# Self-attention products moved behind the scores, into the scores' PSUM ring

## The chip, the cores and the metric

The kernel runs on one core of one Trainium2 chip. A core has five engines with queues of their own: TensorE (PE) multiplies matrices into PSUM, VectorE (DVE), ScalarE (ACT) and GpSimd (POOL) work elementwise, and SyncE (SP) issues DMAs. Each engine executes its own queue in order; between engines semaphores order the work. [...] The metric is the time of one execution on the device in microseconds (us), the median of several runs; less is better.

## The reference

A decoder block in float32, on x of 8 x 224 x 512 and a context of 8 x 750 x 384: self-attention, cross-attention, feed-forward, each with a residual and a layer norm behind it. The change touches the self-attention only:

```python
x = _rmsnorm(tokens, norm_w)
q = x @ Wq
k, v = jnp.split(x @ Wkv, 2, axis=-1)
q, k, v = (split(q), split(k), split(v))      # 16 heads of 64
q = _head_rmsnorm(q, q_gamma)                 # q / max(|q|, 1e-12) * (gamma + 1) * 8
k = _head_rmsnorm(k, k_gamma)
sim = jnp.einsum('bhid,bhjd->bhij', q, k)
sim = jnp.tanh(sim / SOFTCLAMP) * SOFTCLAMP   # 50
attn = jax.nn.softmax(sim * DIM_HEAD ** (-0.5), axis=-1)
out = jnp.einsum('bhij,bhjd->bhid', attn, v)
return out.reshape(b, n, HEADS * DIM_HEAD) @ Wo
x = _layernorm(x + attention)
```

The norm of a head runs over its 64 elements. With the tanh at 50 and the scale of 1/8 the exponent is bounded, so the kernel takes exponentials with no maximum.

## The kernel before

The self-attention works in *slots*, one for each pass of `for m in range(NS)`: NS = 32. Slot m = 8 g + hp handles two batches (group g, G = 448 rows, halves u = 0 and 1 of S = 224) and one pair of heads hp. Within a slot PE does, in program order:

- `self_values(m - 1)` (matmuls on line 577, tile `ov`): exponentials of the slot before by values.
- `self_scores(m)` (line 507, tile `sc_a`): scores of the pair, for each u in a tile of 2 x 512 float32, two banks, from the pool `a_sc`, which has two such buffers. ACT then runs tanh (line 517) and exp (line 523), each in two pieces of keys a half: eight calls.
- `project_v` (line 484, `mm_v`): one tile of values, in 24 of the 32 slots. ACT copies it out (line 494) in one to four pieces, as the row tiles of 128 straddle batches of 224.
- `transpose_xn` (line 342, `tr_x`): a tile of the next group's normalised input, in ten slots. DVE copies it out (`copy_xn`, line 346).
- `products_qk(m + 2)` (line 421; `q_x`, `q_z`, `q_w`): queries and keys for two slots later.
- `self_output` (line 610, `mm_o`): an output tile of the group before, in the slots that the table `out_at` names.

Queries and keys are not computed as one product of 448 x 512 by 512 x 256, but with seven products of half blocks, in `half_products` (Winograd's form): inputs and weights are cut into blocks, POOL prepares four sums of each (`sum_input` line 405, `sum_weights` line 385), and the products accumulate into three PSUM tiles x, z, w. ACT copies an intermediate state out of x three times (`m1` line 259, `u2` line 265, `u4` line 271), before the next product may add to it, and z and w once (c11 line 263, c22 line 269); POOL adds m1 to c11 (line 272) and u4 to c22 (line 273). After a yield, two last products follow, with DVE's c21 (line 278) and ACT's c12 (line 282). x, z and w come from the pool `a_mm`, three banks, which `mm_v`, `tr_x` and `mm_o` use too.

The head norms of queries and keys: ACT squares (`square_qk`, line 447), DVE sums within heads (`head_norms`, lines 454 to 465), POOL takes the power -0.5 (tile `nm_i`, line 167), DVE spreads the result and scales (`scale_qk`, lines 472 and 474). In slot m `head_norms(m + 1)` comes before `scale_qk(m + 1)`; the scores of slot m + 1 need both. `inverse_sums(m)` sums the exponentials on DVE (lines 532 to 563), `weigh(m - 1)` (line 590) scales the values' result.

POOL also computes the sums of weights for each hp (at set slots, `sums_at`), of the inputs of the next group (hp = 5), and, in `room_sums`, of cross-attention weights (line 138). From slot 10 on the blocks of weights come from DRAM with `load_slot`, issued two slots ahead; `room_load` brings in cross-attention weights.

The order of PE, DVE, ACT and POOL instructions is that of the program text (`manual_schedule`). SP's DMAs are placed by the scheduler.

The function `half_products` is also used by the cross-attention, with `third` set and no calls to deal out.

Of the kernel before, what the change touches and what calls it, by code (L numbers as in the profile page):

```python
# [21 lines left out]
F32 = mybir.dt.float32  # L22
# [17 lines left out]
P = 128  # L40
# [24 lines left out]
def decoder_block(ctx: ExitStack, tc: tile.TileContext, a: dict, out: bass.AP):  # L65
# [175 lines left out]

    def half_products(product, a, b, sums_a, sums_b, dest, parts, acc, third=None):

        (a11, a12), (_, a22) = a
        (b11, _), (b21, b22) = b  # L250
        s1, s2, s3, s4 = sums_a
        t1, t2, t3, t4n = sums_b
        c11, c12, c21, c22 = (dest(r, c) for r in range(2) for c in range(2))
        m1, u2, u4 = parts
        x_, z_, w_ = acc
        if third:
            a13, a23, b31, b32, dif = third
        product(x_, a11, b11, True)
        nc.scalar.copy(m1, x_)  # L259
        product(z_, a12, b21, True)  # L260
        if third:
            product(z_, a13, b31, False)
        nc.scalar.copy(c11, z_)
        product(x_, s2, t2, False)
        nc.scalar.copy(u2, x_)
        product(w_, s3, t3, True)
        if third:
            product(w_, a23, b32, False)
        nc.scalar.copy(c22, w_)
        product(x_, s1, t1, False)  # L270
        nc.scalar.copy(u4, x_)
        nc.gpsimd.tensor_tensor(c11, c11, m1, ALU.add)
        nc.gpsimd.tensor_tensor(c22, c22, u4, ALU.add)
        yield
        product(w_, a22, t4n, False)
        if third:
            product(w_, a23, dif, False)
        nc.vector.tensor_tensor(c21, w_, u2, ALU.add)  # L278
        product(x_, s4, b22, False)
        if third:  # L280
            product(x_, a13, b32, False)
        nc.scalar.copy(c12, x_)
        yield
# [15 lines left out]
    with tc.tile_pool(name="a_sb", bufs=2) as sb, tc.tile_pool(  # L299
# [38 lines left out]
        def transpose_xn(i):  # L338
            y = xn.pop(i)
            trs[i] = tr = ps_mm.tile([P, KD, P], F32, tag="mm", name="tr_x")  # L340
            for k in range(KD):
                nc.tensor.transpose(tr[:, k, :], y[:, k * P : (k + 1) * P], ident)
# [80 lines left out]
                    skip_group_check=True,  # L423
                )

        def products_qk(m):
            g, hp = divmod(m, NPAIR)
            qk[m] = sb.tile([P, 2, G], F32, name="qk", bufs=3)
            if m < NPAIR + 2:
                q, k = ([w[:, 2 * kh : 2 * kh + 2, hp * P : (hp + 1) * P] for kh in range(2)]  # L430
                    for w in (wq, wk))
                b = (q[0], None), (q[1], k[1])
                t = [work[:, hp % 4, i] for i in range(4)]
            else:
                w7 = stream[:, m % 2]
                b = (w7[:, 0], None), (w7[:, 1], w7[:, 2])
                t = [w7[:, 3 + i] for i in range(4)]
            return half_products(
                product_qk, input_blocks(g), b, [sums_x[:, i] for i in range(4)], t,
                lambda u, w: qk[m][:, w, u * S : (u + 1) * S],  # L440
                [sb.tile([P, S], F32, name=n, bufs=1) for n in ("qm1", "qu2", "qu4")],
                [ps_mm.tile([P, S], F32, tag="mm", name=f"q_{n}") for n in ("x", "z", "w")],
            )

        def square_qk(m):
# [3 lines left out]
        def head_norms(m):  # L449

            quarter = sb.tile([P, 4 * NB], F32, name="nm_q", bufs=1)
            nc.vector.tensor_reduce(
                quarter, sq_qk[m].rearrange("p w (b c) -> p (w b) c", c=Q32), AX.X, ALU.add,
                apply_transpose=True,
            )
            other = sb.tile([P, 4 * NB], F32, name="nm_o", bufs=1)
            for q in range(P // Q32):
                o = q ^ 1  # L460
                nc.vector.tensor_copy(
                    other[q * Q32 : (q + 1) * Q32], quarter[o * Q32 : (o + 1) * Q32]
                )
            nc.vector.tensor_tensor(quarter, quarter, other, ALU.add)
            nc.vector.tensor_scalar(quarter, quarter, 1e-24, None, ALU.max)  # L465
            inv[m] = sb.tile([P, 2, 2 * NB, 1], F32, name="nm_i")
            rsqrt(inv[m].rearrange("p w b o -> p (w b o)"), quarter)
# [27 lines left out]

        def self_scores(m):

            qT, kT = qk[m][:, 0], qk[m][:, 1]
            scs = []
            for u in range(2):  # L500
                sc = ps_sc.tile([P, 2, 512], F32, name="sc_a")
                sc = sc[:, :, 0 : NT * S].rearrange("p j (t q) -> p j t q", t=NT)
                scs.append(sc)
                for kt, (k0, n) in enumerate(KEYS):
                    for j in range(2):
                        h0, c = j * DH, u * S
                        nc.tensor.matmul(  # L507
                            sc[:n, j, kt, :],
                            lhsT=kT[h0 : h0 + DH, c + k0 : c + k0 + n],
                            rhs=qT[h0 : h0 + DH, c : c + S],  # L510
                            start=True,
                            stop=True,
                        )
            for u in range(2):
                pr, sc = prs[u], scs[u]
                for kt, (_, n) in enumerate(KEYS):
                    nc.scalar.activation(  # L517
                        pr[:n, :, kt], sc[:n, :, kt], AF.Tanh, scale=1.0 / SOFTCLAMP
                    )


                for kt, (_, n) in enumerate(KEYS):
                    nc.scalar.activation(  # L523
                        pr[:n, :, kt], pr[:n, :, kt], AF.Exp, scale=SOFTCLAMP * SCALE
                    )

        def inverse_sums(m):

# [2 lines left out]
            for u in range(2):  # L531
                nc.vector.tensor_reduce(  # L532
                    quarter[:, u, :, :, :, 0].rearrange("p j b t -> p j t b"),
                    prs[u].rearrange("p j t (b c) -> p j t b c", c=Q32),
                    AX.X, ALU.add, apply_transpose=True,
                )


            flat = quarter.rearrange("p u j b t g -> p (u j b t) g")
# [145 lines left out]

        nc.vector.tensor_scalar(gscale, gam, 1.0, DH**0.5, ALU.add, ALU.mult)
        head_norms(0)
        project_v(0, 0)
        project_v(1, 0)
        project_qk(1)  # L690
# [1 line left out]
        head_norms(1)  # L692
        for i in opened[0][2:]:
            project_v(i, 0)
        for i in range(4):
            if i < 2:
                sum_input(0, 2 * i)
                sum_input(0, 2 * i + 1)
            sum_weights(2, i)

        out_at = [(), (2, 3, 5), (0, 2, 4, 6), (3, 4, 5)]

        sums_at = {0: (3,), 1: (4,), 2: (5, 6), 3: (7,), 4: (0,), 6: (1,)}
        for m in range(NS):
            g, hp = divmod(m, NPAIR)
            ahead = opened[g + 1] if g + 1 < NG else ()
            if m > 0:
                self_values(m - 1)
            self_scores(m)

            c = 1 - hp // 4
            tiles = opened[g + hp // 4] if g + hp // 4 < NG else ()
            if hp % 4 < len(tiles):
                project_v(tiles[hp % 4], c)
            turned = ahead[hp - 2] if 2 <= hp < 2 + len(ahead) else None

            behind = turned is not None and turned * P % (2 * G) < G < turned * P % (2 * G) + P
            if turned is not None and not behind:
                transpose_xn(turned)
            for i in due:  # L720
                scales.append(layernorm([i]))
            due.clear()
            if 2 <= m + 1 < NS and m > 0:
                head_norms(m + 1)
            if m > 0:
                weigh(m - 1)
            if turned is not None and not behind:
                copy_xn(turned)
            sums = inverse_sums(m)
            next(sums)  # L730
            products = products_qk(m + 2) if m + 2 < NS else iter(())
            next(products, None)
            if m + 1 < NS:
                scale_qk(m + 1)
            for _ in products:
                pass
            if m + 2 < NS:
                square_qk(m + 2)
            if behind:
                transpose_xn(turned)  # L740
                copy_xn(turned)
            for f in scales:
                f()
            scales.clear()
# [6 lines left out]
            if hp < len(ahead):  # L751
                square(ahead[hp])
                rms_norms(ahead[hp], ahead[hp] + 1)
            if hp == 5 and ahead:
                for i in range(4):
                    sum_input(g + 1, i)
            for p in sums_at.get(m, ()):
                for i in range(4):
                    sum_weights(p, i)
            if m == NPAIR - 1:  # L760
                stream = wpool.tile([P, 2, 7, KD // 2, P], F32, tag="w", name="w_slot")
                load_slot(m + 3)
# [1 line left out]
                room_load(0)  # L764
            if m >= NPAIR - 1 and m + 4 < NS:
                load_slot(m + 4)

            for _ in range({9: 2, 10: 3, 12: 2, 13: 3}.get(m, 0)):
                next(room_steps[m // 12])
            if m == 10:  # L770
                room_load(1)
            if m == NS - 3:
                xw = wpool.tile([P, 2, KC + 2 + NSUM, P], F32, tag="w", name="xw")
# [728 lines left out]
```

## Time and profile before

| what | value |
|---|---|
| median of 3 runs | 1697.95 us (1697.94 to 1701.26) |
| the profiled execution | 1700.17 us, its span 1698.4 us |
| granted TensorE clock, mean | 0.995 |
| PE busy | 1637.3 us, 96% |
| DVE, ACT, POOL busy | 1339.9, 983.8, 895.1 us |
| self-attention's slots | from 39.19 us to about 553 us of the span |
| DMA, mean | 88 GB/s |

In the profile PE is the matmul pipeline and PEld its loading of weights, which overlaps it; ACTq and the like are the sequencers. A row of a timeline gives start and duration in us, engine, line, operation, tiles as `out<-in`, shapes and how many; in brackets the engine's idle time before it and the instruction whose end released it. A float32 matmul of the program appears as two records. A row of a chain has start, duration, engine, tile and line; the chain is followed back from the last instruction, at each step to what released it. Rows of waits read "who <- for whom: total us, times, longest". Idle time of an engine that does not set the pace costs nothing.

### The profile page before, as it was taken

Reading aid. Unit: us, or ns where it says so; the run is one execution under the profiler, and the core shown is the slowest. Engines: PE = TensorE matmul, PEld = TensorE weight load, DVE = VectorE, ACT = ScalarE, POOL = GpSimd, SP = SyncE. Lnnn points to the kernel's source line nnn. Section 1 sums busy time; section 2 is a strip of 40 time slices with the busy share of each in tenths; the row PEclk is TensorE's granted clock in tenths of the full one; section 3 lists DMA queues with packets and bytes.
Section 4 is the critical chain, followed back from the end, with each engine's and each line's share of the span. In section 5 each row is a group of like instructions: output and inputs, shape, how many; then the busy total and the mean of one; then the engine's idle time right before and its main releaser. Section 6 shows DMA issues by size and latency. Waiting matters only on the chain.

```text
span 1698.4 us, 27332 instructions
## 1 busy us (share of the span) xinstructions
PE 1637.3 (96%) x9844; PEld 1151.2 (68%) x9858; DVE 1339.9 (79%) x2813; ACT 983.8 (58%) x1774; POOL 895.1 (53%) x792
## 2 busy tenths in 40 slices
PE   8988999999998999999999999999999999999998
PEld 4666656666653787778678677777777787874443
DVE  2888778677864788788688687798987787896877
ACT  4655545555631576676576576576665565655663
POOL 3685654345432465465466466465565465653244
PEclk9999999999999999999999999999999999999999
DMA  6014333112310533242233233133212112121333
GB/s 235 38 50 165 102 97 102 44 52 64 112 50 1 204 122 124 87 133 87 71 99 112 69 115 112 48 105 112 63 46 73 40 48 92 52 111 27 73 83 105
DMA packets 140071, 149.67 MB, mean 88 GB/s; under 512 B 41120, under 2 KB 106144, under 8 KB 137504
## 3 DMA queue, kind: packets, MB, share of 16 engines
q1 hardware_dynamic: 139936, 147.93, 28.2%
q8 instruction: 78, 1.28, 0.3%
q14 instruction: 57, 0.47, 0.1%
HBM read 122.47 MB, written 16.78 MB: 82 GB/s over the span
## 4 chain that ended last, share of the span: by engine, by line
PE 79%; DVE 11%; ACT 4%; POOL 4%; issue 2%; SPq 0%; DMA 0%; POOLq 0%; ACTq 0%; DVEq 0%
PE sc_c L1048 8%; PE ov_c L1142 8%; PE mm_o L610 6%; PE k_x L1009 6%; PE mm_co L232 6%; PE mm_f L1303 5%; PE v_x L1015 5%; PE mm_q L1024 5%; PE k_w L1009 4%; PE v_w L1015 4%; PE mm_v L484 4%; PE q_x L421 4%; POOL nm_i L167 3%; PE k_z L1009 2%; PE sc_a L507 2%
## 5 line engine op out<-in xcount | busy, mean ns | idle before, releaser
L1132 POOL TENSOR_TENSOR csh<-cpT 125x672 f32<-125x672 f32 x128 | 207.9, 1625 | 161.6 <-DVE cpT L1122 123.9
L1056 ACT COPY cpT<-sc_c 125x448 f32<-125x448 f32 x384 | 173.9, 564 | 77.8 <-PE sc_c L1048 76.3
L167 POOL TENSOR_TENSOR nm_i<-nm_q,mhalf 128x28 f32<-128x28 f32 x32 | 153.3, 4792 | 114.3 <-DVE nm_q L465 114.3
L1130 ACT ACTIVATE cpT<-cpT 125x1344 f32<-125x1344 f32 x128 | 169.2, 1323 | 48.5 <-DVE cpT L1122 40.6
L1122 DVE TENSOR_TENSOR cpT<-cpT,mx_b 125x1344 f32<-125x1344 f32 x128 | 193.2, 1550 | 2.2
L1048 PE MATMUL sc_c<-cqT,ckT 64*125 64x224 f32 x1536 | 172.7, 360 | 5.1 <-DVE cpT L1122 2.9
L1048 PEld LDWEIGHTS sc_c<-cqT,ckT 64*125 64x125 f32 x1536 | 143.0, 183 | 38.7 <-issue 22.0
L1142 PE MATMUL ov_c<-cpT,cv 125*64 125x224 f32 x1536 | 159.4, 357 | 0.0
L1142 PEld LDWEIGHTS ov_c<-cpT,cv 125*64 125x64 f32 x1536 | 104.7, 137 | 47.2 <-issue 10.3
L1058 DVE TENSOR_TENSOR cm<-sc_c,cpT 125x448 f32<-125x448 f32 x128 | 73.9, 619 | 72.2 <-ACT cpT L1056 72.2
L517 ACT ACTIVATE pr<-sc_a 128x448 f32<-128x448 f32 (+1 forms) x128 | 61.7, 535 | 88.4 <-PE sc_a L507 88.3
L1024 PE MATMUL mm_q<-xT,xattn_Wq 128*128 128x224 f32 x512 | 107.3, 353 | 0.0
L484 PE MATMUL mm_v<-wv,xnT 128*128 128x512 f32 x224 | 104.2, 609 | 0.0
L1134 POOL TENSOR_TENSOR csm<-csm,csh 125x224 f32<-125x224 f32 x128 | 97.6, 763 | 10.0
L610 PE MATMUL mm_o<-attn_Wo,oT 128*128 128x512 f32 (+1 forms) x224 | 100.6, 603 | 2.2 <-DVE qk L278 2.2
L1024 PEld LDWEIGHTS mm_q<-xT,xattn_Wq 128*128 128x128 f32 x512 | 94.3, 190 | 8.1
L1133 POOL TENSOR_TENSOR csm<-csh 125x224 f32<-125x224 f32 x128 | 93.6, 731 | 10.0
L232 PE MATMUL mm_co<-xattn_Wo,coT 128*128 128x512 f32 (+1 forms) x256 | 98.6, 594 | 0.0
L1303 PE MATMUL mm_f<-ternary,xqT 128*128 128x512 bf16 x435 | 97.6, 379 | 0.7
L1303 PEld LDWEIGHTS <-xqT 128*128 128x128 bf16 x448 | 43.8, 98 | 53.2 <-issue 0.6
L421 PE MATMUL q_x<-x_sums,w_slot 128*128 128x224 f32 x264 | 62.6, 360 | 17.4 <-ACT qm L259 14.3
L532 DVE TRANSPOSE_TENSOR_REDUCE sm_q<-pr 128x28 f32<-128x896 f32 x64 | 68.6, 1096 | 13.2 <-ACT pr L523 13.2
(209 smaller groups left out, 3697.0 us busy)
## 6 DMA issues: line engine op xcount, KB each, us to landing
xw<-w_sums SPq DMA_DIRECT2D x64, 320.0 KB, 3.0
w_slot<-qk_sums SPq DMA_DIRECT2D x22, 512.0 KB, 3.7
w_stage<-w_gateT SPq DMA_DIRECT2D x8, 1024.0 KB, 5.1
w_stage<-w_upT SPq DMA_DIRECT2D x8, 1024.0 KB, 5.0
w_stage<-w_downT SPq DMA_DIRECT2D x8, 1024.0 KB, 5.6
xw<-xattn_Wk SPq DMA_DIRECT2D x32, 192.0 KB, 2.6
xw<-xattn_Wv SPq DMA_DIRECT2D x32, 192.0 KB, 2.5
tern<-w_t SPq DMA_DIRECT2D x24, 256.0 KB, 2.1
```

The costliest lines, as they stand in the source:

```text
L167: nc.gpsimd.tensor_tensor(y, v, mhalf.to_broadcast([P, v.shape[-1]]), ALU.pow)
L232: nc.tensor.matmul(mm[row : row + m, :], lhsT=oT[:, k, at : at + m], rhs=w[:, k, :], start=(k == 0), stop=(k == NPAIR - 1),)
L484: nc.tensor.matmul(mm, lhsT=xnT[:, k, at : at + P], rhs=wv[:, k, c * 512 : (c + 1) * 512], start=(k == 0), stop=(k == KD - 1),)
L610: nc.tensor.matmul(mm[row : row + lhsT.shape[-1], :], lhsT=lhsT, rhs=wo[:, hp, :], start=(hp == 0), stop=(hp == NPAIR - 1),)
L1009: nc.tensor.matmul(mm, lhsT=w, rhs=c, start=start, stop=True, skip_group_check=True)
L1024: nc.tensor.matmul(mm, lhsT=xwq[:, k, hp * P : (hp + 1) * P], rhs=xT[:, k, :], start=(k == 0), stop=(k == KD - 1),)
L1048: nc.tensor.matmul(sc[j][:, i, :], lhsT=kT[h0 : h0 + DH, ct * CT : (ct + 1) * CT], rhs=qT[h0 : h0 + DH, :], start=True, stop=True,)
L1056: nc.scalar.copy(pT[:, j, 2 * c2 : 2 * c2 + 2, :], sc[j])
L1122: nc.vector.tensor_tensor(pT[:, j], pT[:, j], nm[:CT, j] .rearrange("p (o q) -> p o q", o=1) .to_broadcast([CT, NCT, S]), ALU.add,)
L1132: nc.gpsimd.tensor_tensor(half, pT[:, j, 0:3], pT[:, j, 3:6], ALU.add)
L1142: nc.tensor.matmul(ov[h0 : h0 + DH, :], lhsT=v[:, ct, hq * DH : (hq + 1) * DH], rhs=pT[:, j, ct, :], start=(ct == 0), stop=(ct == NCT - 1),)
L1303: nc.tensor.matmul(mm, lhsT=xqTs[i][:, k, :], rhs=w[:, k, cols], start=(k == 0), stop=(k == KD - 1),)
```

## The change

Nothing is computed differently; work is ordered otherwise, and PSUM is dealt out otherwise.

- `products_qk` takes x and z from the scores' pool: they are the two banks of one buffer of `a_sc` (tag `sc`), so each slot takes three buffers from that ring of two: scores u = 0, scores u = 1, x and z. Only w stays in `a_mm`.
- In a slot `products_qk(m + 2)` comes right after `self_scores(m)`. `self_scores` no longer issues the eight tanh and exp calls, it returns them; `half_products` issues three of them ahead of the first product, three after m1's copy, one each ahead of the third product's successors w and s1. With such calls, c11 is copied last and POOL adds c22 first.
- Transpose and value tile come after the products.
- `head_norms(m + 2)` closes slot m, after the value tile, in place of `head_norms(m + 1)` near its beginning. `weigh(m - 1)` moves ahead of the products. `inverse_sums` yields after its first half, so that `scale_qk(m + 1)` stands between the two halves' sums.
- Sums of weights: those of hp = 2 and of the first input go before the first value tiles; the others come one set a slot in slots 0 to 6, ahead of the products. The cross-attention's sums are spread over slots 10 to 13 and 15 to 18, the second of its loads goes from slot 10 to slot 13.
- The last group's output tiles are at hp = 3, 5, 6 in place of 3, 4, 5.

```diff
-    def half_products(product, a, b, sums_a, sums_b, dest, parts, acc, third=None):
+    def half_products(product, a, b, sums_a, sums_b, dest, parts, acc, third=None, fill=None):
+        def filling(n):
+            for _ in range(n if fill else 0):
+                fill.pop(0)()
+        between = bool(fill)
...
+        filling(3)
         product(x_, a11, b11, True)
         nc.scalar.copy(m1, x_)
+        filling(3)
         product(z_, a12, b21, True)
...
-        nc.scalar.copy(c11, z_)
+        if not between:
+            nc.scalar.copy(c11, z_)
         product(x_, s2, t2, False)
         nc.scalar.copy(u2, x_)
+        filling(1)
         product(w_, s3, t3, True)
...
         nc.scalar.copy(c22, w_)
+        filling(1)
         product(x_, s1, t1, False)
         nc.scalar.copy(u4, x_)
-        nc.gpsimd.tensor_tensor(c11, c11, m1, ALU.add)
-        nc.gpsimd.tensor_tensor(c22, c22, u4, ALU.add)
+        if between:
+            nc.gpsimd.tensor_tensor(c22, c22, u4, ALU.add)
+            nc.scalar.copy(c11, z_)
+            nc.gpsimd.tensor_tensor(c11, c11, m1, ALU.add)
+        else:
...
-        def products_qk(m):
+        def products_qk(m, calls):
+            pair = ps_sc.tile([P, 2, 512], F32, tag="sc", name="q_xz")
+            w_ = ps_mm.tile([P, S], F32, tag="mm", name="q_w")
...
-                [ps_mm.tile([P, S], F32, tag="mm", name=f"q_{n}") for n in ("x", "z", "w")],
+                [pair[:, 0, :S], pair[:, 1, :S], w_],
+                fill=calls,
...
-        out_at = [(), (2, 3, 5), (0, 2, 4, 6), (3, 4, 5)]
-        sums_at = {0: (3,), 1: (4,), 2: (5, 6), 3: (7,), 4: (0,), 6: (1,)}
+        out_at = [(), (2, 3, 5), (0, 2, 4, 6), (3, 5, 6)]
         for m in range(NS):
...
-            self_scores(m)
+            calls = self_scores(m)
+            if m > 0:
+                weigh(m - 1)
+            for i in due:
+                scales.append(layernorm([i]))
+            due.clear()
+            if m < NPAIR - 1:
+                for i in range(4):
+                    sum_weights((m + 3) % NPAIR, i)
+            for _ in range({10: 1, 11: 1, 12: 1, 13: 2, 15: 1, 16: 1, 17: 1, 18: 2}.get(m, 0)):
+                next(room_steps[m // 15])
+            products = products_qk(m + 2, calls) if m + 2 < NS else iter(())
+            next(products, None)
+            for f in calls:
+                f()
+            sums = inverse_sums(m)
+            next(sums)
+            if m + 1 < NS:
+                scale_qk(m + 1)
+            for _ in products:
+                pass
+            next(sums)
+            if m + 2 < NS:
+                square_qk(m + 2)
+            if 2 <= hp < 2 + len(ahead):
+                transpose_xn(ahead[hp - 2])
+                copy_xn(ahead[hp - 2])
+            if hp == 5 and ahead:
+                for i in range(4):
+                    sum_input(g + 1, i)
             c = 1 - hp // 4
             tiles = opened[g + hp // 4] if g + hp // 4 < NG else ()
             if hp % 4 < len(tiles):
                 project_v(tiles[hp % 4], c)
...
-            if 2 <= m + 1 < NS and m > 0:
-                head_norms(m + 1)
...
             if m + 2 < NS:
-                square_qk(m + 2)
...
+                head_norms(m + 2)
...
-            if m == 10:
+            if m == 13:
                 room_load(1)
```

More of the change, by code (lines that the diff above doesn't have):

```diff
@@ L269, in half_products @@
         nc.scalar.copy(c22, w_)
+        filling(1)
         product(x_, s1, t1, False)
         nc.scalar.copy(u4, x_)
-        nc.gpsimd.tensor_tensor(c11, c11, m1, ALU.add)
-        nc.gpsimd.tensor_tensor(c22, c22, u4, ALU.add)
+        if between:
[3 more added lines that the diff above has]
+        else:
+            nc.gpsimd.tensor_tensor(c11, c11, m1, ALU.add)
+            nc.gpsimd.tensor_tensor(c22, c22, u4, ALU.add)
         yield
@@ L500, in self_scores @@
             for u in range(2):
-                sc = ps_sc.tile([P, 2, 512], F32, name="sc_a")
+                sc = ps_sc.tile([P, 2, 512], F32, tag="sc", name="sc_a")
                 sc = sc[:, :, 0 : NT * S].rearrange("p j (t q) -> p j t q", t=NT)
@@ L513, in self_scores @@
                         )
+            calls = []
             for u in range(2):
                 pr, sc = prs[u], scs[u]
[L516 to L525, printed above, removed]
+                for y, f, by in ((sc, AF.Tanh, 1.0 / SOFTCLAMP), (pr, AF.Exp, SOFTCLAMP * SCALE)):
+                    for kt, (_, n) in enumerate(KEYS):
+                        calls.append(partial(
+                            nc.scalar.activation, pr[:n, :, kt], y[:n, :, kt], f, scale=by
+                        ))
+            return calls
         def inverse_sums(m):
@@ L536, in inverse_sums @@
                 )
+                if u == 0:
+                    yield
             flat = quarter.rearrange("p u j b t g -> p (u j b t) g")
@@ L687, in decoder_block @@
         head_norms(0)
+        for i in range(4):
+            if i < 2:
+                sum_input(0, 2 * i)
+                sum_input(0, 2 * i + 1)
+            sum_weights(2, i)
         project_v(0, 0)
@@ L694, in decoder_block @@
             project_v(i, 0)
[L695 to L699, printed above, removed]
-        out_at = [(), (2, 3, 5), (0, 2, 4, 6), (3, 4, 5)]
-        sums_at = {0: (3,), 1: (4,), 2: (5, 6), 3: (7,), 4: (0,), 6: (1,)}
+        out_at = [(), (2, 3, 5), (0, 2, 4, 6), (3, 5, 6)]
         for m in range(NS):
@@ L708, in decoder_block @@
                 self_values(m - 1)
-            self_scores(m)
+            calls = self_scores(m)
[26 more added lines that the diff above has]
+            if hp == 5 and ahead:
+                for i in range(4):
+                    sum_input(g + 1, i)
             c = 1 - hp // 4
@@ L714, in decoder_block @@
                 project_v(tiles[hp % 4], c)
[L715 to L722, printed above, removed]
-            if 2 <= m + 1 < NS and m > 0:
-                head_norms(m + 1)
[L725 to L736, printed above, removed]
             if m + 2 < NS:
-                square_qk(m + 2)
-            if behind:
-                transpose_xn(turned)
-                copy_xn(turned)
+                head_norms(m + 2)
             for f in scales:
@@ L753, in decoder_block @@
                 rms_norms(ahead[hp], ahead[hp] + 1)
[L754 to L759, printed above, removed]
             if m == NPAIR - 1:
@@ L766, in decoder_block @@
                 load_slot(m + 4)
-            for _ in range({9: 2, 10: 3, 12: 2, 13: 3}.get(m, 0)):
-                next(room_steps[m // 12])
-            if m == 10:
+            if m == 13:
                 room_load(1)
```

## The prediction

> **What bounds the kernel now.** I read the page first, then the waits of the self-attention (0 to 500 us), then one slot of it in order of time, then the chain at its end. A *slot* is one pass of the loop over `m`; its start is the first score matmul (line 507). Slot 0 starts at 39.19 us and slot 31 at 518.57; cross-attention, untouched, starts at about 553.
>
> The page's parts 1 and 4:
>
> ```profile
> PE 1637.3 (96%) x9844; PEld 1151.2 (68%) x9858; DVE 1339.9 (79%) x2813; ACT 983.8 (58%) x1774; POOL 895.1 (53%) x792
> PE 79%; DVE 11%; ACT 4%; POOL 4%; issue 2%; SPq 0%; DMA 0%; POOLq 0%; ACTq 0%; DVEq 0%
> ```
>
> TensorE is the bound, but 96% is a mean over stages. The page says nothing of where the remainder sits, so I asked for the waits (columns: total us, times, longest):
>
> ```profile
> POOL nm_i L167 <- DVE nm_q L465: 112.6, 30, 13.0
> ACT pr L517 <- PE sc_a L507: 72.6, 19, 10.5
> DVE sq_qk L472 <- POOL nm_i L167: 40.3, 26, 4.9
> PE q_x L421 <- ACT qm L259: 19.0, 16, 1.8
> PE sc_a L507 <- DVE qk L474: 6.1, 5, 2.3
> ```
>
> The large waits belong to POOL and ACT and cost nothing in themselves. The two PE lines do: products wait for the copy `qm`, scores wait for scaled queries and keys. Why `qm` is late, from slot 9 (start us, duration):
>
> ```profile
> 167.78 0.97 ACT L517 ACTIVATE pr<-sc_a 128x448 f32<-128x448 f32 x2 [0.65 <-PE sc_a L507]
> 168.42 3.70 PE L484 MATMUL mm_v<-wv,xnT 128*128 128x512 f32 x8
> 170.42 1.04 ACT L523 ACTIVATE pr<-pr 128x448 f32<-128x448 f32 x2
> 172.16 2.34 ACT L494 COPY v<-mm_v 32x512 f32<-32x512 f32 x4 [0.69 <-PE mm_v L484]
> 174.52 0.34 ACT L259 COPY qm<-q_x 128x224 f32<-128x224 f32 x1
> 174.92 1.02 PE L421 MATMUL q_x<-x_sums,w_slot 128*128 128x224 f32 x4 [1.28 <-ACT qm L259]
> ```
>
> ACT does eight tanh and exp, then the value tile's copies, and only then `qm`; PE stands for 1.28. Slots 27 to 29 have no value tile to hide the exponentials, and each stands for 1.55. The chain at the end shows the other kind of wait:
>
> ```profile
> 507.74 1.03 DVE nm_q L454
> 510.13 4.77 POOL nm_i L167
> 514.93 1.17 DVE sq_qk L472 x2
> 516.10 2.33 DVE qk L474 x2
> 518.57 3.36 PE sc_a L507 x16
> ```
>
> Slot 30 has neither products nor an output tile, so the norm (started inside that slot) is bare: PE stands 5.68 before slot 31. And the clock, in two windows after long waits (us of PE, PEld, DVE, ACT, POOL, then PE clock):
>
> ```profile
> 152.00:157.00 5.00, 4.64 (x19) 2.68 (x20) 4.70 (x15) 4.37 (x9) 0.00 (x0) 0.67 1.00 368
> 518.00:523.00 5.00, 4.43 (x22) 3.03 (x24) 4.73 (x12) 2.53 (x6) 1.25 (x1) 0.57 0.00 0
> ```
>
> [...] sixteen score matmuls take 3.36 us at 518.57 and 2.14 at 152.36, against 1.71 elsewhere in the chain; [...] x and z become halves of a 2 x 512 f32 tile, one bank each, so z may still be written while x is copied; [...] a weight sum (line 385) takes 0.73, but 1.11 at 108.41 beside L474, which takes 1.84 instead of 1.24.
>
> **PE's work in a slot.** From the chain's pieces: values 1.67 (L577), scores 1.71, seven products of four records 7 x 0.76 = 5.32, value tile 3.65, 0.23 of joints: 12.58, which is what slots 9, 21, 25, 26 show (13.86 less 1.28). An output tile adds 6.87, a transposed input tile 0.44; a slot without value tile has 8.93.
>
> **The change, part by part.**
>
> *Products behind the scores.* Count from the first score matmul. Tanh starts at 1.07 (166.71 to 167.78), the pair ends at 2.04. x and z now take the buffer of the first scores, so x waits for that pair: PE stands from 1.71 to 2.10 (a release costs about 0.06: 174.86 to 174.92). Then, with pitches 0.43 for tanh, 0.47 for exp, 0.24 for a copy, 0.76 for a product, and 1.06 from a product's start after idling to its copy (0.96 otherwise): x 2.10; z 2.96; copy m1 3.16 to 3.50; s2 3.75; exp, tanh, tanh 3.40 to 4.73; u2 4.73 to 5.07; w 4.51; s1 5.27; c22 5.47 to 5.82; a22 6.03; u4 6.23 to 6.57; last product 6.79 to 7.55. Without a wait it would be 1.71 + 5.32 = 7.03, with joints about 7.1. So 0.45 a slot is left, in place of up to 1.28 or 1.55. ACT and PE run neck and neck here: if a copy's pitch is its whole 0.345 I get 0.6; if all eight exponentials stayed ahead, 1.3.
>
> *Value tile, transposes and their copies go to the end.* Value copies start 3.74 after L484, at 11.2; the next tanh is ready at 13.03 + 1.07 = 14.1. Four copies (2.34) end at 13.5 and are hidden. With `scale_x` (0.70) and `square` (0.80) behind them, ACT is free at 15.0: 0.96 late, in slots 2 and 9 alone; elsewhere fewer copies or an output tile cover it. Lost: 1.9. If cover were gone everywhere, each value-tile slot would pay its ACT tail.
>
> *Norms at a slot's end.* Squares start at 8.1 (after the two POOL adds, 6.6 to 7.9, and c12), norms on DVE 9.7 to 11.9, the root on POOL to 16.7, which is 3.7 in the next slot; DVE wants it at 5.1, after the first sum. Scaling ends at 7.5, and scores need it at 13.0: 5 us of slack where before there was none. Queued behind the root on POOL: 0.56 of row norm, 0.24 tail copy, four weight sums (2.9 to 3.6), then the adds, at 7.7 to 9.2 in slots 1 to 6; square, value copies and tanh stand behind these on ACT, still in time. Slot 5's input sums (4 x 1.14) push one root to 6.0 of slot 6; slack covers it.
>
> *Early weight sums.* 4 x 1.14 + 4 x 0.72 = 7.4 on POOL, in its idle 27.9 to 36.0 before the second root: nothing. Without that hole the second root is late by as much, and needed only by slot 1.
>
> *DMAs.* Slot 7's stream loads leave when z is done, at 3.7, land about 3.1 and 6.0 later (142.59 to 145.64, 143.58 to 149.55), at 6.8 and 10.7; slot 8's products want them at 11.5 and 13.0. Xattn_Wk, Wo queue behind and have three slots. `room_load(1)` three slots later still has one before its use (6.5 to land). Nothing on the path.
>
> *Output tile from slot 28 to 30.* Slot 28 becomes a bare 9.4; slot 30 gets 6.87 of work in place of 7.3 of waiting, and root 31 is now issued in slot 29. Slot 30: 1.71 + 6.87 + 1.67 = 10.3.
>
> **The sum.** Before, slots 0 to 30: 518.57 - 39.19 = 479.4. After: 30 x (8.93 + 0.45) + 24 value tiles x 3.65 + 10 outputs x 6.87 + 10 transposes x 0.44 + 3.5 (slot 30's scores and values) + 1.9 = 281.4 + 87.6 + 68.7 + 4.4 + 3.5 + 1.9 = 447.5. Gain 31.9; slot 31's scores at full clock, 3.36 - 1.71 = 1.65. Together 33.5. As a check, PE's idle times in its timeline over these slots add up to 41.3, and two half-clock stretches cost about 1.7 each. The profiled execution took 1700.17 (span 1698.4), the median is 2.2 lower: 1700.2 - 33.5 = 1666.7, or 1664.5 by the median. I say 1666, leaving a little for the copy pitch.
>
> **Rivals.**
> - *Partial (0.22).* ACT sets the pace inside the products: gap 1.3, not 0.45: 30 x 0.85 = 25.5 lost, gain 8, 1690; halfway, 1678. For it: ACT's pitches and PE's are within 0.1. Against: only two ACT calls stand ahead of most copies.
> - *Slower (0.08).* POOL's 4.79 root slips ahead of the two adds. Square then starts at 12.9, and with 0.95, 1.7 of value copies and 0.75 behind it tanh is 2.2 late in the 18 slots with a value tile and no output tile: 40 lost, 1706. It decides against the change from 1.86 late, so from a square at 12.6. Against: my root ends at 3.7 to 6.0, the adds start at 6.6 or later.
> - *No effect (0.02).* Gains and the tails on ACT cancel within 0.2% (3.4 us), about what this measurement can tell from no change.
> - *As worked out (0.68)*: 1656 to 1674.
>
> Faster by over 0.2% is 0.68 + 0.22 = 0.90; within, 0.02; slower, 0.08. For 8 in 10 the range takes the likeliest case and the upper half of partial: 1657 to 1684. Below 1657 PE would need to lose its 0.45 too (30 x 0.45 = 13.5).
>
> **What would show it.** Right: slot starts 13.0 to 13.1 apart where there is a value tile; q_x waiting about 0.4 for a tanh once a slot, and hardly at all for `qm`; no half-clock stretch between 60 and 500 us; slot 28 about 9.4, slot 30 about 10.3. Wrong: q_x waiting for `qm` or `qu` by over 0.3 each, tanh preceded by copies or `sq_x` on ACT with PE idle, or a root directly before the POOL adds.

## The result, and the profile after

| | before | after |
|---|---|---|
| median of 4 runs, us | 1698.53 (1697.94 to 1701.26) | 1684.11 (1683.09 to 1685.05) |
| ratio | | 0.991 (0.9895 to 0.9929) |
| profiled execution, us | 1700.17, span 1698.4 | 1683.09, span 1681.3 |
| slots 0 to 30, us | 479.38 | 466.69 |

The kernel is faster by 14.4 us, 0.9%. The prediction was 1666, so the direction was right and the gain was less than half of what was worked out; the time lies 0.1 beyond the upper end of the range, 1684.

The page of the kernel after, parts 1 and 4:

```profile
PE 1638.8 (97%) x9858; PEld 1147.1 (68%) x9858; DVE 1323.8 (79%) x2813; ACT 981.7 (58%) x1774; POOL 896.9 (53%) x792
PE 89%; DVE 5%; ACT 4%; issue 1%; DMA 0%; POOL 0%; SPq 0%; POOLq 0%; ACTq 0%; DVEq 0%
```

TensorE has the same work; its share of the chain that ended last rises from 79% to 89%, DVE's falls from 11% to 5% and POOL's from 4% to nothing. The long way of the norms is off the path.

TensorE's own waits of the kernel after, between 0 and 500 us (for whom, total us, times, longest):

```profile
PE q_xz L437 <- ACT qm L266: 13.0, 30, 0.4
PE q_xz L437 <- ACT pr L252: 12.3, 30, 1.4
```

Before there were several kinds of wait, each in some slots: 19.0 us for `qm` in 16, 6.1 for scaled keys in 5, and smaller ones for DVE and POOL. After there are these two (what else the view holds is in the prologue), and each comes in all 30 slots that have products: 0.4 for `qm`, and 0.3 for the tanh pair, longer in three. Scores wait for queries and keys no more. The prediction counted on the second line and not on the first. One slot shows why; TensorE from the start of slot 25 (423.73) on. The duration of a group includes a modelled end that overlaps the next; go by the starts:

```profile
423.73 1.78 PE L527 MATMUL sc_a<-qk 64*128 64x224 f32 x16
425.82 1.02 PE L437 MATMUL q_xz<-xnT,w_slot 128*128 128x224 f32 x4 [0.31 <-ACT pr L252]
427.28 1.02 PE L437 MATMUL q_xz<-xnT,w_slot 128*128 128x224 f32 x4 [0.43 <-ACT qm L266]
428.14 0.92 PE L437 MATMUL q_xz<-x_sums,w_slot 128*128 128x224 f32 x4
...
431.26 1.02 PE L437 MATMUL q_xz<-x_sums,w_slot 128*128 128x224 f32 x4
432.12 3.60 PE L503 MATMUL mm_v<-wv,xnT 128*128 128x512 f32 x8
```

ACT in the same slot:

```profile
424.80 0.97 ACT L252 ACTIVATE pr<-sc_a 128x448 f32<-128x448 f32 x2 [1.47 <-PE sc_a L527]
...
426.89 0.34 ACT L266 COPY qm<-q_xz 128x224 f32<-128x224 f32 x1 [0.65 <-PE q_xz L437]
...
430.86 0.35 ACT L285 COPY qk<-q_xz 128x224 f32<-128x224 f32 x1
```

Product x starts 2.09 into the slot, as worked out (2.10). Product z is to follow 0.86 later. It follows 1.46 later, 0.05 after ACT has copied x away, though it writes the other bank. ACT is not late: it stood 0.65 for x to be finished. So ACT waits for TensorE to finish x, and then TensorE waits for ACT to copy it. The same happens once more: the slot's last product (431.26) follows 0.05 after ACT has copied c11 out of z (430.86 and 0.35), though it writes into x.

The chain of the kernel after, in slot 30 and at the start of slot 31 (start, duration, engine, tile and line):

```profile
495.18 1.71 PE sc_a L527 x16
496.89 7.06 PE mm_o L631 x16
503.96 1.67 PE ov_a L598 x16
505.63 1.71 PE sc_a L527 x16
```

Slot 30 has no gap at all, and slot 31's scores run at full clock (1.71, before 3.36). Two windows that answer those of before, at the start of slot 8 and of slot 31 (us of PE, PEld, DVE, ACT, POOL, then clock, DMA share, GB/s):

```profile
147.00:152.00 5.00, 4.25 (x31) 3.15 (x27) 4.53 (x15) 3.09 (x8) 2.46 (x1) 1.00 0.98 359
505.50:510.50 5.00, 5.00 (x34) 2.54 (x34) 4.18 (x9) 3.69 (x8) 1.80 (x3) 1.00 0.00 0
```

The granted clock is 1.00 where it was 0.67 and 0.57.

Where the 12.69 us of slots 0 to 30 come from, by the starts of the score matmuls:

| slots | before, us | after, us | gained |
|---|---|---|---|
| 0 to 3 | 57.18 | 57.01 | 0.2 |
| 4 to 10 | 104.93 | 100.58 | 4.4 |
| 11, 12 | 30.57 | 31.49 | -0.9 |
| 13 | 24.20 | 20.90 | 3.3 |
| 14 to 26 | 198.72 | 202.06 | -3.3 |
| 27 to 30 | 63.78 | 54.65 | 9.1 |

Slots 4 to 10 and 13 had waits for norms, `qm` and c21 and, in slots 8 and 13, half-clock stretches (granted clock 0.67 from 152 to 157 us and 0.84 from 246 to 256; in the kernel after 1.00 from 40 to 520). In slots 14 to 26 the kernel before had some slots with no wait to remove: slot 24 took 12.70 and takes 13.59. Slots that had stood 1.28 for `qm` went from 13.86 only to 13.59. Slots 27 to 30 hold most of the gain, and 8.05 of it is in slots 28 and 30, between which an output tile was moved.

### The profile page after: what moved, and what is told of

It reads as the page before. It is cut to its first block, busy times and chain, and to the rows that moved or that the text cites. A ratio compares the mean times of both kernels' runs of the same rounds, so it can differ in the third digit from the quotient of the medians.

```text
span 1681.3 us, 27353 instructions
## 1 busy us (share of the span) xinstructions
PE 1638.8 (97%) x9858; PEld 1147.1 (68%) x9858; DVE 1323.8 (79%) x2813; ACT 981.7 (58%) x1774; POOL 896.9 (53%) x792
## 3 DMA queue, kind: packets, MB, share of 16 engines
q8 instruction: 78, 1.28, 0.3%
## 4 chain that ended last, share of the span: by engine, by line
PE 89%; DVE 5%; ACT 4%; issue 1%; DMA 0%; POOL 0%; SPq 0%; POOLq 0%; ACTq 0%; DVEq 0%
PE sc_c L1064 9%; PE ov_c L1158 8%; PE q_xz L437 8%; PE k_x L1025 6%; PE mm_o L631 6%; PE v_x L1031 6%; PE mm_co L232 6%; PE mm_v L503 6%; PE mm_f L1319 6%; PE mm_q L1040 5%; PE k_w L1025 5%; PE v_w L1031 4%; PE ov_a L598 3%; PE q_w L437 3%; PE k_z L1025 2%; PE v_z L1031 2%
## 5 line engine op out<-in xcount | busy, mean ns | idle before, releaser
L252 ACT ACTIVATE pr<-sc_a 128x448 f32<-128x448 f32 x120 | 57.9, 534 | 73.5 <-PE sc_a L527 73.4
L503 PE MATMUL mm_v<-wv,xnT 128*128 128x512 f32 x224 | 100.4, 592 | 0.0
L513 ACT COPY v<-mm_v 32x512 f32<-32x512 f32 (+2 forms) x80 | 46.2, 577 | 58.0 <-PE mm_v L503 57.4
```

Source lines behind the costliest of these rows:

```text
L503: nc.tensor.matmul(mm, lhsT=xnT[:, k, at : at + P], rhs=wv[:, k, c * 512 : (c + 1) * 512], start=(k == 0), stop=(k == KD - 1),)
```

## The experiments

**Theory A:** z waits because x and z are one tile of the program, whose accesses are kept in order as a whole; the bank has nothing to do with it. **Theory B:** ACT sets the pace inside the products (the rival "partial"). The first experiment gives z a tile of its own; x stays in the scores' ring, with its wait for tanh:

```diff
-            pair = ps_sc.tile([P, 2, 512], F32, tag="sc", name="q_xz")
-            w_ = ps_mm.tile([P, S], F32, tag="mm", name="q_w")
+            pair = ps_sc.tile([P, 2, 512], F32, tag="sc", name="q_x")
+            z_, w_ = (ps_mm.tile([P, S], F32, tag="mm", name=f"q_{n}") for n in "zw")
...
-                [pair[:, 0, :S], pair[:, 1, :S], w_],
+                [pair[:, 0, :S], z_, w_],
```

> The changed kernel, with one edit: z is a tile of its own in the pool a_mm; x keeps the scores' buffer (one bank of it unused). Theory A (a tile is one thing for the waits: because x and z are halves of one tile, z's product waits for m1's copy of x, and the last product waits for c11's copy of z): both waits vanish, a value-tile slot goes from 13.59 to 13.0-13.1 us, 30 slots x 0.55 = 16 us less: 1666 to 1669 us. Theory B (ACT itself cannot keep pace between exponentials and copies, the tile is innocent): z no longer waits but the next products wait for u2 and u4 instead; slot 13.4 to 13.6, 1679 to 1684 us.

Measured: 1663.51 us (1662.63 to 1664.04), ratio to before 0.979 (0.9778 to 0.9807). TensorE in the slot that starts at 406.72, the same slot 25:

```profile
406.72 1.78 PE L527 MATMUL sc_a<-qk 64*128 64x224 f32 x16
408.82 1.02 PE L437 MATMUL q_x<-xnT,w_slot 128*128 128x224 f32 x4 [0.31 <-ACT pr L252]
409.68 0.92 PE L437 MATMUL q_z<-xnT,w_slot 128*128 128x224 f32 x4
...
414.22 3.60 PE L503 MATMUL mm_v<-wv,xnT 128*128 128x512 f32 x8
```

The wait for `qm` is gone and the slot takes 12.70 in place of 13.59. With the order of all instructions unchanged, 0.60 of the 0.89 is z's start (the wait of 0.43, and about 0.16 by which a product that need not wait starts ahead of the modelled end of the group before: 0.86 after the start of a group of 1.02). The rest is in the starts behind the other products of the shared tile: 0.10 at s2, 0.18 around the last product, which in the kernel after waits in the same way for c11's copy out of z. Theory A stands and B falls: ACT has the same calls in the same order. The traces also show that it is the program that waits: in the kernel after, already the first weight load of product z waits for ACT's `qm` (0.78 in slot 25; 23.5 us in 30 slots); in this run no product of z has a wait, in any of the 30 slots. Only slot 7 is worse, 14.94 in place of 10.16, with a wait of 2.94 for tanh and a half-clock stretch of 6.83.

The second experiment takes x out of the ring too, `z_, x_, w_` all from `a_mm`, to measure the tanh wait:

> The changed kernel, but x, z and w are three tiles of a_mm as in the kernel before (allocated z, x, w); the scores' ring holds scores alone; the order of all work is the changed one. Theory A: the false waits go and also the 0.31 us for the first tanh, since x no longer takes the first scores' buffer: slot 12.7 us, 30 x 0.87 = 26 us less: 1657 to 1661 us. If a bank of a_mm is now missing (tr_x or mm_v waits for c12's copy of x), 0.3 to 0.9 a slot comes back: 1665 to 1684. Theory B: 1675 to 1684.

1659.30 us (1658.11 to 1660.29), 0.977 (0.9754 to 0.9786). The basic slot, one with a value tile and nothing else beside its products, is 12.31 and has no wait on TensorE; the 0.39 against 12.70 is just what the prediction gave for x standing behind tanh. A new one appears: in five slots (2, 4, 10, 13 and 18) the value tile waits, 5.8 us in all, for DVE's c21, which holds one of the three banks of `a_mm`. All five also have a transposed tile, one more taker of these banks. `qm` is still waited for in five slots, 4.5 us in all, 1.88 of it in slot 7.

**Dealing out the exponentials.** All eight ahead of m1's copy, nothing else changed:

```diff
-        filling(3)
+        filling(8)
         product(x_, a11, b11, True)
         nc.scalar.copy(m1, x_)
-        filling(3)
         product(z_, a12, b21, True)
```

(The two later `filling(1)` go too.)

> The changed kernel, but all eight tanh and exp calls stand ahead of m1's copy on ACT, none between the copies. Theory A: m1 is copied at 1.07 + 3.58 = 4.65 after the first score instead of 3.16, and z waits for it: each slot 1.4 longer than 13.59 less what the later copies save (the queue behind m1 is short, so c22 and u4 are no longer late): +0.9 to +1.4 a slot, 1710 to 1726 us. Theory B (ACT's total is the pace): the order of its calls would not matter much, 1684 to 1695.

1775.56 us (1773.21 to 1777.2), 1.045 (1.0436 to 1.0467): slower than both kernels, and by far more than expected. Slot 15 (from 306.61 on), TensorE:

```profile
308.70 1.02 PE L434 MATMUL q_xz<-xnT,w_slot 128*128 128x224 f32 x4 [0.31 <-ACT pr L252]
311.65 1.75 PE L434 MATMUL q_xz<-xnT,w_slot 128*128 128x224 f32 x4 [1.92 <-ACT qm L266]
313.19 1.70 PE L434 MATMUL q_xz<-x_sums,w_slot 128*128 128x224 f32 x4
```

The wait for `qm` grows from 0.43 to 1.92, the 1.5 that was expected. But behind it come products of 1.75 and 1.70 in place of 1.02 and 0.92: the clock is halved for 3.41 us (in slot 3 for 6.83), in 27 of the 30 slots (granted clock 0.92 over the first 500 us, in the kernel after 1.00). Such a slot takes 16.76; the slots 1 and 25, which have the same wait and no half clock, take 15.08, which is 13.59 and 1.5. So of the 3.17 a slot half is the clock. (Slot 7, the third without half clock, takes 11.65 in place of 10.16, the same 1.5 more.)

**The output tile alone.** The kernel before with the one line of the table changed:

```diff
-        out_at = [(), (2, 3, 5), (0, 2, 4, 6), (3, 4, 5)]
+        out_at = [(), (2, 3, 5), (0, 2, 4, 6), (3, 5, 6)]
```

> The kernel before with one edit: the last group's second output tile at hp = 6 instead of hp = 4. If that one move carries half of the measured gain: slot 28 falls from 17.57 to 10.7 (like slot 23, which has neither value nor output tile), slot 30 stays at 11.1 as its wait for the root takes the 6.87 of output work: 6.9 us less, 1691 to 1692 us. If the end of the phase is set by the norms alone, 1697 to 1699.

1691.31 us (1690.19 to 1692.21), 0.9956 (0.9941 to 0.9971), as expected. Its chain at slot 30:

```profile
501.89 7.06 PE mm_o L610 x16
508.95 1.67 PE ov_a L577 x16
510.62 1.71 PE sc_a L507 x16
```

It is the same picture as in the kernel after: the tile covers the norm. One number in a table gives 6.9 us, about half of what the whole change gives, if it is all that is changed. The reverse, the kernel after with the old table:

> The changed kernel, with the last group's output tiles at hp = 3, 4, 5 again. With root 31 issued a slot early, slot 30 without output work is not bare: slot 28 rises from 10.16 to 17.0, slot 30 falls from 10.45 to about 6.7: 3.1 us more, 1687 us. If the end still waits for the root as before, 6.9 more, 1691.

1690.08 us (1688.43 to 1694.21), 6.0 above the kernel after. In its profile slots 0 to 30 take 470.39 in place of 466.69, 3.7 more where 3.1 were expected: slot 28 takes 17.03 as worked out, slot 30 takes 7.21 and not 6.7. So with the norms issued earlier the same table entry is worth about half as much. Most of the remainder lies behind slot 31, in code that is the same in both: from slot 31's start to the end it takes 1175.8 in the profiles of the kernel after and of two other runs here, and 1178.0 to 1178.2 in this and seven others. (In the kernel before it takes 1179.8; the further 1.8 are slot 31's scores at half clock.) So some 2 us of a comparison of single profiles can come from there.

**Norms at a slot's end.** The kernel after with the norm back ahead of the value's scaling in the following slot:

```diff
+            if 2 <= m + 1 < NS:
+                head_norms(m + 1)
             if m > 0:
                 weigh(m - 1)
...
-            if m + 2 < NS:
-                head_norms(m + 2)
```

> The changed kernel, with the head norms of slot m + 1 back at the beginning of slot m, ahead of weigh, instead of those of m + 2 at its end. If the placing at the end is worth little by itself because the chain norm, root, scaling (2.2 + 4.8 + 2.4 = 9.5 us from the slot's start) fits into a slot of 13.6: full slots unchanged, slots 1 to 6 later by up to 2 each as the sums and adds now queue behind the root: 1686 to 1694 us. If the early norm is what carries the change, every slot lengthens and the end shows the long wait again: over 1700.

1712.89 us (1711.48 to 1713.86), 1.008 (1.0066 to 1.0096): slower than the kernel before, 28.8 above the kernel after, and well above what was expected. ACT in slot 5's end and slot 6's start (128.05):

```profile
129.42 0.95 ACT L466 ACTIVATE sq_qk<-qk 128x896 f32<-128x896 f32 x1 [6.02 <-POOL qk L286]
...
132.76 0.97 ACT L252 ACTIVATE pr<-sc_a 128x448 f32<-128x448 f32 x2
```

POOL ahead of it:

```profile
119.55 4.79 POOL L167 TENSOR_TENSOR nm_i<-nm_q,mhalf 128x28 f32<-128x28 f32 x1 [6.22 <-DVE nm_q L484]
...
128.73 0.66 POOL L286 TENSOR_TENSOR qk<-qk,qm 128x224 f32<-128x224 f32 x1
```

The root (`nm_i`) stands in front of the weight sums and the two adds, and it starts 5.9 after the beginning of slot 5, where in the kernel after it starts 1.2 ahead of it. The square waits for the adds, the value copies stand behind the square on ACT and tanh behind these. Later, where POOL has no weight sums left, the square waits for DVE's c21 instead (4.28 in slot 25), which stands behind the scaling, and this behind the root. TensorE waits 1.7 to 3.95 for tanh in slots 3, 6, 7, 10, 25 and 26, with half-clock stretches behind the four longest of these waits, in slots 3, 6, 7 and 10 (granted clock of the whole execution 0.994, in the kernel after 0.998). A late root that makes tanh late is the mechanism of the prediction's slower rival. The forecast rested on the place of the norm, and that place is worth 28.8 us in this order of the products.

**Towards a better version.** With x, z and w in `a_mm`, `scale_x` and `square` of the row norms moved from the end of the slot to just behind `square_qk`, ahead of the value copies on ACT:

```diff
             if m + 2 < NS:
                 square_qk(m + 2)
+            if 1 <= hp < 1 + len(ahead):
+                scale_x(ahead[hp - 1])
+            if hp < len(ahead):
+                square(ahead[hp])
```

> x, z and w as three tiles of a_mm (the run before), and scale_x and square of the next input tile moved on ACT from the slot's end to right behind square_qk, ahead of the value tile's copies. If ACT's tail at the slot's end is what makes tanh late in the slots after a full one (slots 3 and 10 of the changed kernel wait 1.28 and 1.39 instead of 0.31), those waits vanish and 2 to 3 us are gained on 1659.3: 1656 to 1658. If those slots are late because of POOL's adds, nothing: 1659.

1658.77 us (1657.85 to 1658.88), 0.976 (0.9747 to 0.9777), 0.5 below the run without this, which is less than the spread of either. The waits that it is about are gone from slots 3 and 9 and smaller in 10, but slot 7 now gets a half-clock stretch, behind a wait of 1.9 for `qm`, and the value tile waits 6.7 us for c21:

```profile
PE mm_v L502 <- DVE qk L294: 6.7, 6, 1.6
```

That the move took the waits away is not shown for slots 9 and 10: the next run keeps the move, has no such stretch in slot 7, and there they are 0.67 and 1.25, nearly what they were without the move (0.67 and 1.37). ACT's square in slot 8 waits 4.31 for c21 without the move and again in the next run, and 2.94 in this one. One suspect for the value tile's waits and for slot 7 was POOL, with the weight sums ahead of the adds in slots 0 to 6. Moved behind them (the same loop over `sum_weights`, after `next(products, None)`):

> As the run e5_xzw_tail, and the sums of weights of slots 0 to 6 stand on POOL behind the two adds of the products, not ahead of them. If square_qk (and with it value copies and tanh) waits in slots 1 to 7 for adds that stand behind these sums, slot 7's wait (1.88 with x, z, w in a_mm) and mm_v's waits in slots 2 and 4 go: 3 to 5 us under e5, 1652 to 1655. If POOL's root itself is what is late, no change.

1660.97 us (1659.67 to 1661.45), 0.9775 (0.976 to 0.979): a miss, 2.2 above the run with the move alone. ACT in slot 6 and POOL beside it:

```profile
130.74 0.95 ACT L465 ACTIVATE sq_qk<-qk 128x896 f32<-128x896 f32 x1 [4.73 <-DVE qk L294]
```

```profile
122.56 4.79 POOL L167 TENSOR_TENSOR nm_i<-nm_q,mhalf 128x28 f32<-128x28 f32 x1 [0.92 <-DVE nm_q L483]
...
128.11 0.66 POOL L286 TENSOR_TENSOR qk<-qk,qm 128x224 f32<-128x224 f32 x1
```

The adds are done by 128.8, and the square starts at 130.74 all the same: it now waits for DVE's c21, which stands on DVE behind the scaling, which waits for the root, which ends at 127.35. The sums were not what came last.

If it is w's bank that the value tile lacks, w can go where its late release hurts nobody: into the scores' ring, x and z into `a_mm`; `scale_x` and `square` stay behind `square_qk`.

```diff
-            pair = ps_sc.tile([P, 2, 512], F32, tag="sc", name="q_xz")
-            w_ = ps_mm.tile([P, S], F32, tag="mm", name="q_w")
+            pair = ps_sc.tile([P, 2, 512], F32, tag="sc", name="q_w")
+            z_, x_ = (ps_mm.tile([P, S], F32, tag="mm", name=f"q_{n}") for n in "zx")
...
-                [pair[:, 0, :S], pair[:, 1, :S], w_],
+                [x_, z_, pair[:, 0, :S]],
```

> Kernel after with the three product tiles dealt the other way round: z and x from the banks of the value tiles, w, which no product needs before 4.5 us of a slot, from the scores' ring; and scale_x and square behind square_qk as in the run before with that tail. Against that run (1658.8 us): its basic slot stays at 12.31, since w's buffer is free at 2.1 and wanted at 3.7 or later. Its six waits of the value tile for DVE's c21 (1.35, 0.60, 0.89, 1.63, 1.00 and 1.19, together 6.7 us) go, because the bank that c21 holds is no longer one that a value tile or a transposed tile takes; the late c21 then holds a scores' buffer which is wanted only 3 us later. Slot 7's wait of 1.9 for qm with its half clock stays. If this is right: 1652 (1650 to 1654). If these waits came from DVE being late for the transposed tile's own copies rather than from the bank that w holds, the value tile is as late as before: 1657 to 1660.

1653.23 us (1652.97 to 1653.5), 0.973 (0.9718 to 0.975): as expected, and the best version here, 45.3 us below the kernel before (1698.51 beside it) and 30.9 below the kernel after. All that TensorE waits for in the slots up to 500 us:

```profile
PE q_x L437 <- ACT qm L266: 6.3, 5, 2.9
```

25 of the 30 slots with products have no wait; five wait for `qm`, of which slot 7 (2.87, and a half-clock stretch) is the longest. The value tile's six waits for c21 are gone, as worked out; those for `qm` have grown from 3.0 to 6.3, so part of the 6.7 comes back there. The cause of slot 7's wait was looked for in the root standing behind slot 5's four input sums on POOL; they were moved behind `head_norms`:

> As the run with w in the scores' ring, and the four input sums of slot 5 (and 13, 21) behind head_norms instead of ahead of it, so that POOL takes the root for slot 7 before the sums. If slot 7's wait (1.9 us, and about 1.9 more through the half clock behind it) comes from the root standing behind the sums on POOL: slot 7 falls from 12.7 to about 8.9, 3.8 us less than the run it is set against, 1648. If it comes from the weight sums and adds on POOL that stand ahead of slot 6's square whatever the root does: no change, 1652. If the sums, moved into slot 6's beginning, hold up slot 6's two adds instead, slot 6 or 7 waits by 2 to 4 us and the gain is gone.

1661.47 us (1660.26 to 1663.04), 0.978 (0.9769 to 0.9798), 8 us worse, and none of the three outcomes: slot 7 does fall to 8.90 with no wait, but slot 6 takes 22.31, since its third product needs those sums. Nearest is the third outcome, but it is the product that waits, not the two adds, and for 6.79. Slot 22 loses in the same way: it takes 25.82 in place of 19.18, with a wait of 3.37 for its sums and half clock behind it. Slot 14 does not; slot 13 ahead of it has an output tile, so POOL has 7.3 us longer.

```profile
125.93 1.86 PE L437 MATMUL q_x<-x_sums,w_room 128*128 128x224 f32 x4 [6.79 <-POOL x_sums L421]
```

As slot 6 stands 6.79 for the sums, everything behind it has time to catch up, so the run does not tell what slot 7 had waited for. That stays open.

## Why the prediction was right and wrong

Its sum for slots 0 to 30 was 447.5; measured 466.69, 19.2 too little. By its own terms:

| term | predicted | measured | error over the slots |
|---|---|---|---|
| slot without value tile | 8.93 + 0.45 = 9.38 | 10.16 | 30 x 0.78 = 23.4 |
| value tile | 3.65 | 13.59 - 10.16 = 3.43 | 24 x -0.22 = -5.3 |
| output tile, transposed tile | 6.87, 0.44 | 6.87, 0.44 | 0 |
| ACT's tail | 1.9 | 0.81 + 0.97 + 1.08 = 2.9 | 1.0 |
| slot 30 | 10.37 | 10.45 | 0.1 |

Of the 0.78 in the first line the shared tile makes 0.90 (10.16 against 9.26 with z in a tile of its own); all else in the slot was put 0.12 too high.

**The step that failed** is the sentence that x and z are halves of one tile, "one bank each, so z may still be written while x is copied", and with it "0.45 a slot is left". Writing z while x is copied is what the first experiment shows: with z in a tile of its own, in another bank, z's product starts at 409.68 and goes on while ACT copies x (409.88 to 410.23), and nothing is lost. But the kernel waits by tile: with one tile for both, z's first matmul stands until x's copy has ended (0.43), and the last product until z's has. The prediction asked whether the two accesses may overlap, not what the program waits for, and here the second set the time. The other starts follow from this one:

| start after the scores, us | x | z | s2 | w | a22 | last product | next work |
|---|---|---|---|---|---|---|---|
| predicted | 2.10 | 2.96 | 3.75 | 4.51 | 6.03 | 6.79 | 7.55 |
| kernel after | 2.09 | 3.55 | 4.41 | 5.17 | 6.69 | 7.53 | 8.39 |
| z in its own tile | 2.10 | 2.96 | 3.72 | 4.47 | 5.99 | 6.74 | 7.50 |

With the one tile undone, the prediction's schedule is met to 0.05 at every start. So ACT's and TensorE's pitches, the tanh term of 0.39, and the dealing out were sized rightly. That slots 0 to 30 then take 445.92, against 447.5, is in part luck: a basic slot takes 12.70 and not the 13.03 of the sum, 7.9 less over the 24 slots with a value tile, and slot 7's 5.7 of waiting and half clock, which were not forecast, take most of that back.

The value tile's 3.65 was read too high. Before's own trace has the number: slot 23, without one, takes 10.70 with a wait of 1.55, so 9.15, and 12.58 less 9.15 is 3.43. The 12.58 was too high as well: a slot that waits for nothing takes 12.31 in the second experiment. The two errors nearly cancel in the 8.93 for a slot without value tile, which measures 8.88 there. That is luck too.

**Behind slot 31's start** it gave 1.65 and the profile shows 4.05 (17.06 of span less 13.0). 1.8 of this is there when the cross-attention first applies its values (58.93 behind slot 31's start in the kernel before, 57.10 in the kernel after), so the half clock was sized rightly. The other 2.2 comes later in the cross-attention, which the change does not touch. It is the difference of some 2 us between the profiles named above; what makes it is not known.

**Right:** no half-clock stretch between 60 and 500 us (granted clock 1.00); ACT's tail in slots 2 and 9 makes the next tanh late by 0.97 and 1.08 (0.96 given), while slot 0, with the prologue's value copies ahead of it, was not thought of; norms with slack, as scores never wait for scaled queries; early weight sums and DMAs at no cost; the output tile, though slot 28 is 10.16 and not 9.4. The sign named for being wrong, products that wait for `qm` "by over 0.3 each", is what came: 0.43 in each of 30 slots.

**The rivals.** "Partial" had a time that fits (1678 to 1690) for a reason that does not: ACT does not set the pace, as the first experiment shows. The slower rival's mechanism is real when the root is put there; it was priced at 2.2 in each of 18 slots, and comes as 1.7 to 3.95 in six and as about 1 or less in the others.

## What to carry to other kernels

When two results share a tile, ask what the program waits for, not only what the memory allows: two halves in different banks were serialised at 0.6 to 0.9 us a slot, and giving one of them a tile of its own brought 20.6 us more, where the whole change with the shared tile, its moved output tile included, had brought 14.4. Put the accumulator whose release is latest into the ring that is wanted latest (here 5.5 us). A reordering that replaces waits of some slots by a fixed wait in every slot must be counted over the slots that had none.

## What the runs showed of the hardware

The price of a wait on TensorE was not only its length. With all eight exponentials ahead of m1's copy, each of the 30 slots had a wait of 1.92 for `qm`. In 27 of them the clock was halved behind it, for 3.41 us (once 6.83), with products of 1.75 and 1.70 in place of 1.02 and 0.92; such a slot took 16.76. Slots 1 and 25, with the same wait and no half clock, took 15.08, so the half clock cost 1.7. Slot 7 had none either, at 11.65 in place of 10.16. What set these three apart is not shown.

In the kernel before, the waits of 2.33 ahead of slot 8 and of 5.68 ahead of slot 31 went with scores of 2.14 and 3.36 in place of 1.71. In the kernel after, whose longest wait in a slot is 1.39, the granted clock is 1.00 from 40 to 520 us.
